# A cross-attention block on one core: another order of the steps that lead into the steady loop

## The chip, the cores and the metric

The kernel runs on one core of a Trainium2 chip. A core has five engines that run side by side, each through its own queue of instructions in order: TensorE (PE, with its weight loads PEld), VectorE (DVE), ScalarE (ACT), GpSimd (POOL) and SyncE (SP), which here only issues DMA transfers. An instruction that has to wait for another engine holds up everything behind it in its own queue. The metric is the device time of the whole kernel in microseconds (us).

## What is computed

Sixteen images x of 1024 rows and 512 features attend to 64 context rows each. All in 32-bit floats:

```python
def _ada_ln(x, c, W_ss, b_ss):
    mu = jnp.mean(x, axis=-1, keepdims=True)
    var = jnp.mean((x - mu) ** 2, axis=-1, keepdims=True)
    h = (x - mu) / jnp.sqrt(var + EPS)
    ss = jax.nn.silu(c) @ W_ss + b_ss
    scale, bias = jnp.split(ss, 2, axis=-1)
    return (1.0 + scale)[:, None, :] * h + bias[:, None, :]
xq = _ada_ln(x_q, t_vec, Wss_q, bss_q)
xkv = _ada_ln(x_kv, t_vec, Wss_kv, bss_kv)
q = (xq @ Wq + bq).reshape(B, Lq, nh, dh)
kv = (xkv @ Wkv + bkv).reshape(B, Lkv, 2, nh, dh)
k, v = kv[:, :, 0], kv[:, :, 1]
scores = jnp.einsum('bqhd,bkhd->bhqk', q, k) / jnp.sqrt(jnp.float32(dh))
attn = jax.nn.softmax(scores, axis=-1)
out = jnp.einsum('bhqk,bkhd->bqhd', attn, v).reshape(B, Lq, H)
return x_q + (out @ Wp + bp)
```

There are 16 heads of 32 features.

## The kernel before

**Blocks.** The rows of x are cut into 32 blocks of 512 rows; a block is four tiles of 128 rows. The context is handled in two groups, "A" and "B", of eight images (512 context rows) each. The three dense layers (query, key and value, output) are computed as products of half-size matrices with seven products in place of eight: `query_product(i, n)`, `context_product(g, "k" or "v", n)` and `product(i, n)` stand for product n of 1 to 7, each four matmul calls (L521, L937). For this the kernel forms sums and differences of weight halves (`column_sums`, `weight_sums`, on POOL) and of feature halves (`feature_sums`, `row_sums`, mostly on POOL). Block 0 is projected without this, by `project_seeded` (L868).

**One block's way.** `load_x` brings the block (SP); `q_stats` (DVE) and `q_scale` (ACT and POOL) make mean and inverse deviation; `hidden` normalises it (ACT); `turn` transposes 32x32 squares (DVE, into the tile `ht`, of which there is one); `move` exchanges the squares between partitions by sixteen transfers from `ht` to `xt` on SP's queue (for block 1, with `two=True`, eight on SP and eight on POOL); `scale_features` applies the conditioning (ACT, four steps). Then the seven query products (PE) and `query_out` (ACT) and `query_added` (DVE) take the query to `qt`, a single buffer. `score_products(i, z)` makes the scores of one half z of the keys into two double banks of PSUM; `maximum` (DVE) and `copied` (ACT) take them out, and only then can the next half go there. `maxima` spreads the row maxima (`mb`), `subtract` (POOL), `weights` (ACT, the exponential), `total` (POOL) and `row_total` (DVE) follow; `inverse_rows` takes the inverse sums through DRAM (`ltd`) back in another order (`vr`) by five small transfers on SP; `spread_rows` and `divided` (DVE) apply them to the result of `mix` (PE), and `product` with `added`, or for block 0 `project_seeded` with `projected`, project it, add it to the residual that `load_residual` brought, and store it. Seeds of the projection's banks are written by ACT (`project_seed`, `biased`).

**The first block and the context** take shorter ways: block 0 and the context rows are transposed on PE (`turned_products`, `turned_features`), and the context is scaled by `modulated` (half on DVE, half on ACT). The conditioning itself comes from `scale_shift_rows`, `scale_shift_taken` and `scale_shift`, with `biases` transposing the bias rows. Values are stored to a stage and brought to their place by `value_move`, eight transfers each.

**The order** is written out by hand, step by step, from L992 on: 410 steps up to L1402, then a loop over the blocks 3 to 29 (L1404), then the last blocks. No scheduler moves anything: a step's instructions go to the end of each engine's queue in the order of the calls. Buffers are shared by tags with few copies: the tag "x" has two for the rows of x, and "r" two for the residuals, which at first hold the value weights and their sums (L159 and L160); a load into a buffer waits for its last reader.

Of the kernel before, what the change touches and what calls it, by code (L numbers as in the profile page):

```python
# [20 lines left out]
def cross_attention_block(  # L21
# [18 lines left out]
    nc = tc.nc  # L40
# [289 lines left out]
    def q_scale(i):  # L330
        apart = i != "A"
        q_rstd[i] = rstd_of(q_mv.pop(i), NT, apart)
# [669 lines left out]
    column_sums("k", w_k_sb, w_k_sums, (2,))  # L1002
    turned_features("A", 0)
    scale_shift_taken("kv", 0)
    hidden("A", (2,))
    column_sums("k", w_k_sb, w_k_sums, (0,))
    turned_features("A", 1)
    turned_features("A", 2)
    scale_shift("kv", 2 * NC, 0)
    column_sums("v", w_v_sb, wv_sums, (2,))  # L1010
    column_sums("v", w_v_sb, wv_sums, (0,))
    turned_features("A", 3)
    modulated("A", 0, 0, nc.scalar)
    load_x("B")
    column_sums("k", w_k_sb, w_k_sums, (1,))
    column_sums("v", w_v_sb, wv_sums, (1,))
    modulated("A", 0, 0, nc.vector)
    scale_shift_rows("kv", 1)
    modulated("A", 0, 1, nc.scalar)
    context_product("A", "k", 1)  # L1020
    column_sums("v", w_v_sb, wv_sums, (3,))
    scale_shift_taken("kv", 1)
    column_sums("k", w_k_sb, w_k_sums, (3,))
    modulated("A", 0, 1, nc.vector)
    scale_shift("kv", 2 * NC, 1)
    modulated("A", 1, 0, nc.vector)
    modulated("A", 1, 0, nc.scalar)
    modulated("A", 1, 1, nc.vector)
    modulated("A", 1, 1, nc.scalar)
    context_out("A", "k", 1)  # L1030
    context_product("A", "v", 1)
    context_product("A", "k", 2)
    context_out("A", "v", 1)
    feature_sums("A", nc.vector, (0,))
    context_out("A", "k", 2)
    feature_sums("A", nc.vector, (1,))
    load_query_weights()
    context_product("A", "v", 2)
    context_out("A", "v", 2)
    feature_sums("A", nc.vector, (2,))  # L1040
    context_product("A", "k", 7)
    feature_sums("A", nc.vector, (3,))
    context_product("A", "v", 7)
    context_out("A", "v", 7)
    context_product("A", "k", 6)
    q_stats(0, (0,))
    context_product("A", "v", 6)
    q_stats(0, (1,))
    context_out("A", "k", 7)
    context_out("A", "k", 6)  # L1050
    q_stats(0, (2,))
    q_stats(0, (3,))
    q_stats("B", (0,))
    q_scale(0)
    scale_shift_rows("q", 0)
    hidden(0, (0,))
    scale_shift_rows("q", 1)
    context_product("A", "k", 5)
    q_stats("B", (1,))
    hidden(0, (1,))  # L1060
    context_out("A", "v", 6)
    context_product("A", "k", 4)
    context_product("A", "v", 5)
    column_sums("q", w_q_sb, w_q_sums, (0,))
    hidden(0, (2,))
    hidden(0, (3,))
    load_x(1)
    q_stats("B", (2,))
    scale_shift_taken("q", 0, 2)
    q_stats("B", (3,))  # L1070
    q_scale("B")
    hidden("B", (1,))
    scale_shift("q", 0, 0, 2)
    context_out("A", "k", 5)
    turned_products()
    turned_scaled(0)
    hidden("B", (0,))
    turned_scaled(3)
    turned_scaled(1)
    turned_scaled(2)  # L1080
    context_product("A", "k", 3)
    context_out("A", "v", 5)
    feature_sums(0, nc.gpsimd, (0,))
    hidden("B", (2,))
    load_projection_bias()
    column_sums("q", w_q_sb, w_q_sums, (2,))
    context_product("A", "v", 4)
    context_out("A", "k", 3)
    hidden("B", (3,))
    turned_features("B", 0)  # L1090
    modulated("B", 0, 0, nc.vector)
    turned_features("B", 1)
    context_product("A", "v", 3)
    turned_features("B", 2)
    modulated("B", 1, 0, nc.scalar)
    feature_sums(0, nc.gpsimd, (1,))
    context_out("A", "k", 4)
    column_sums("q", w_q_sb, w_q_sums, (1,))
    query_product(0, 1)
    modulated("B", 0, 0, nc.scalar)  # L1100
    query_seed(0)
    turned_features("B", 3)
    q_stats(1, (0,))
    q_stats(1, (1,))
    context_out("A", "v", 3)
    feature_sums(0, nc.gpsimd, (2,))
    q_stats(1, (2,))
    load_x(2)
    modulated("B", 0, 1, nc.scalar)
    q_stats(1, (3,))  # L1110
    load_projection()
    query_product(0, 2)
    context_product("B", "k", 1)
    feature_sums(0, nc.gpsimd, (3,))
    column_sums("q", w_q_sb, w_q_sums, (3,))
    query_product(0, 6)
    modulated("B", 1, 1, nc.scalar)
    context_out("A", "v", 4)
    modulated("B", 0, 1, nc.vector)
    modulated("B", 1, 1, nc.vector)  # L1120
    q_scale(1)
    modulated("B", 1, 0, nc.vector)
    query_out(0, 2)
    feature_sums("B", nc.gpsimd, (0,))
    context_out("B", "k", 1)
    hidden(1, (0,))
    feature_sums("B", nc.gpsimd, (1,))
    query_product(0, 7)
    context_product("B", "k", 2)
# [9 lines left out]
    query_out(0, 6)  # L1139
    load_x(3)  # L1140
    context_out("B", "k", 2)
    q_stats(2, (0,))
    query_out(0, 7)
    q_stats(2, (1,))
    move(1, two=True)
    q_stats(2, (2,))
    context_product("B", "k", 6)
    context_out("B", "k", 6)
    query_product(0, 5)
    query_product(0, 4)  # L1150
    value_move("A", 0)
    q_stats(2, (3,))
    query_added(0, 5)
    q_stats(3, (0,))
    q_stats(3, (1,))
    q_scale(2)
    query_product(0, 3)
    value_move("A", 1)
    context_product("B", "k", 7)
    context_product("B", "k", 5)  # L1160
    q_stats(3, (2,))
    query_added(0, 4)
    hidden(2, (0,))
    hidden(2, (1,))
    hidden(2, (2,))
    query_out(0, 3)
    context_out("B", "k", 7)
    q_stats(3, (3,))
    hidden(2, (3,))
    turn(2, (0,))  # L1170
    load_x(4)
    turn(2, (1,))
    turn(2, (2,))
    scale_features(1, (0,))
    nc.gpsimd.tensor_tensor(b_diff, b_second, b_first, ALU.subtract)
    scale_features(1, (3,))
    scale_features(1, (2,))
    scale_features(1, (1,))
    feature_sums(1, nc.gpsimd, (0,))
    feature_sums(1, nc.gpsimd, (1,))  # L1180
    score_products(0, 0)
    context_product("B", "k", 4)
    maximum(0, 0, 0)
    context_out("B", "k", 5)
    query_product(1, 1)
    copied(0, 0, 1)
    maximum(0, 0, 1)
    turn(2, (3,))
    copied(0, 0, 0)
    context_out("B", "k", 4)  # L1190
    query_seed(1)
    q_scale(3)
    score_products(0, 1)
    maximum(0, 1, 1)
    context_product("B", "k", 3)
    maximum(0, 1, 0)
    feature_sums(1, nc.gpsimd, (2,))
    hidden(3, (3,))
    query_product(1, 2)
    context_out("B", "k", 3)  # L1200
    context_product("B", "v", 1)
    query_out(1, 2)
    query_product(1, 6)
    move(2)
    copied(0, 1, 0)
    query_product(1, 7)
    context_out("B", "v", 1)
    maxima(0)
    copied(0, 1, 1)
    feature_sums(1, nc.gpsimd, (3,))  # L1210
    context_product("B", "v", 2)
    query_out(1, 6)
    q_stats(4, (0,))
    query_out(1, 7)
    context_out("B", "v", 2)
    context_product("B", "v", 6)
    context_out("B", "v", 6)
    context_product("B", "v", 7)
    subtract(0, zs=(0,))
    q_stats(4, (1,))  # L1220
    subtract(0, zs=(1,))
    hidden(3, (0,))
    hidden(3, (1,))
    weights(0, 0)
    turn(3, (0,))
    weights(0, 1)
    scale_features(2, (1,))
    total(0)
    hidden(3, (2,))
    q_stats(4, (2,))  # L1230
    query_product(1, 5)
    scale_features(2, (3,))
    query_product(1, 4)
    turn(3, (1,))
    scale_features(2, (2,))
    context_product("B", "v", 5)
    query_added(1, 5)
    context_out("B", "v", 7)
    q_stats(4, (3,))
    query_added(1, 4)  # L1240
    scale_features(2, (0,))
    turn(3, (2,))
    context_out("B", "v", 5)
    query_product(1, 3)
    context_product("B", "v", 4)
    load_x(5)
    turn(3, (3,))
    query_out(1, 3)
    feature_sums(2, nc.gpsimd, (0,))
    row_total(0)  # L1250
    inverse_rows(0)
    move(3)
    score_products(1, 0)
    maximum(1, 0, 0)
    copied(1, 0, 1)
    copied(1, 0, 0)
    context_out("B", "v", 4)
    maximum(1, 0, 1)
    query_product(2, 1)
    score_products(1, 1)  # L1260
    maximum(1, 1, 0)
    maximum(1, 1, 1)
    load_residual(1)
    q_scale(4)
    context_product("B", "v", 3)
    load_residual(0)
    query_seed(2)
    maxima(1)
    feature_sums(2, nc.gpsimd, (1,))
    context_out("B", "v", 3)  # L1270
    feature_sums(2, nc.gpsimd, (2,))
    copied(1, 1, 0)
    copied(1, 1, 1)
    project_seed(0, 1)
    query_product(2, 2)
    query_out(2, 2)
    hidden(4, (0,))
    mix(0)
    subtract(1, zs=(0,))
    spread_rows(0)  # L1280
    query_product(2, 6)
    hidden(4, (2,))
    project_seed(0, 0)
    query_out(2, 6)
    hidden(4, (1,))
    value_move("B", 1)
    divided(0)
    q_stats(5, (0,))
    subtract(1, zs=(1,))
    weights(1, 0)  # L1290
    hidden(4, (3,))
    q_stats(5, (1,))
# [320 lines left out]
```

## Time and profile before

| | |
|---|---|
| median of 3 runs | 1034.3 us (1032.55 to 1035.55) |
| profiled execution, first to last instruction | 1029.1 us |
| busy: PE | 1009.3 us (98%) |
| busy: PEld | 763.4 us (74%) |
| busy: DVE | 860.9 us (84%) |
| busy: POOL | 805.9 us (78%) |
| busy: ACT | 638.6 us (62%) |
| moved by DMA | 149.82 MB, mean 146 GB/s |

The profiler took down one execution: each instruction with its engine, its line in the kernel, its start and its end. The page groups them; other views list one engine's instructions in order of time, the waits with what ended them, the transfers from issue to landing, or the busy time in chosen stretches. Times in the views are microseconds from the first instruction on, unless marked ns. A name such as `pq<-xt,w_q_sb` says what is written and what is read; equal names stand for different blocks, since buffer numbers are left out. The granted clock is the share of full speed that TensorE was given.

### The profile page before, as it was taken

How to read it: one execution, taken by the hardware profiler on the slowest of the kernel's cores; microseconds unless marked ns; L12 is line 12 of the kernel's file. 1: busy time of each engine (PE TensorE's matmuls, PEld its weight loads, DVE VectorE, ACT ScalarE, POOL GpSimd, SP SyncE). 2: the span in 40 equal slices, each digit the busy share in tenths (PEclk: the TensorE clock that was granted, in tenths of full speed). 3: DMA queues.
4: the chain of work that ended last, by engine and by line, in shares of the span. 5: the costliest groups of instructions: out<-in, count | busy, mean ns of one | idle time of the engine just before them, and what ended most of it. 6: DMA issues, size and time to landing. Idle time of an engine off the chain costs nothing.

```text
span 1029.1 us, 21212 instructions
## 1 busy us (share of the span) xinstructions
PE 1009.3 (98%) x8077; PEld 763.4 (74%) x8077; DVE 860.9 (84%) x1174; ACT 638.6 (62%) x1025; POOL 805.9 (78%) x518
## 2 busy tenths in 40 slices
PE   8999899999999999999999999999999999999998
PEld 7877556777777777777777778777777777777746
DVE  6686669889888888889898888898888888876795
ACT  3786565666666666667666666666666676665530
POOL 4566687798888888898888888988888888987861
PEclk9999999999999999999999999999999999999999
DMA  9563544444544444445444444445434444335122
GB/s 318 179 188 119 149 122 136 157 157 156 165 155 121 143 128 154 152 152 166 140 134 146 150 133 153 156 159 165 148 110 151 134 154 154 113 125 166 46 85 85
DMA packets 112197, 149.82 MB, mean 146 GB/s; under 512 B 34104, under 2 KB 45392, under 8 KB 112096
## 3 DMA queue, kind: packets, MB, share of 16 engines
q1 hardware_dynamic: 111712, 147.94, 45.3%
q8 instruction: 64, 1.05, 0.4%
q0 software_dynamic: 384, 0.54, 0.3%
q14 instruction: 37, 0.30, 0.1%
HBM read 79.21 MB, written 34.60 MB: 111 GB/s over the span
## 4 chain that ended last, share of the span: by engine, by line
PE 81%; SPq 6%; DMA 5%; DVE 4%; ACT 1%; issue 1%; POOL 1%; DVEq 0%; ACTq 0%; POOLq 0%
PE pp L955 34%; PE pq L539 33%; PE po L826 6%; PE ps L658 6%; SPq L387 4%; DMA ltd<-lt 1%; SPq L631 1%; PE pk_A L539 1%; PE pv_A L539 1%; DMA xt<-ht 1%; DMA r<-in_x_dram 1%; DVE ht L365 1%; DVE lt L762 1%; DMA wss_kv<-in_L_xcond_Wss_kv_dram 1%; DMA x<-in_x_dram 1%
## 5 line engine op out<-in xcount | busy, mean ns | idle before, releaser
L717 POOL TENSOR_TENSOR s<-s,mb 128x2048 f32<-128x2048 f32 x64 | 290.2, 4558 | 129.3 <-DVE mb L704 127.7
L684 ACT COPY s<-ps 128x1024 f32<-128x1024 f32 x128 | 129.4, 1012 | 108.1 <-DVE m L675 64.8
L675 DVE TRANSPOSE_TENSOR_REDUCE m<-ps 128x32 f32<-128x1024 f32 x128 | 150.7, 1213 | 33.6 <-PE ps L658 33.4
L955 PE MATMUL pp<-w_p_sb,ot 128*128 128x256 f32 x720 | 165.6, 379 | 0.5 <-DVE r L979 0.4
L979 DVE TENSOR_TENSOR r<-pp,r 128x512 f32<-128x512 f32 x203 | 131.8, 670 | 30.9 <-PE pp L955 24.3
L578 ACT ACTIVATE qt<-pq,bias_t 128x256 f32<-128x256 f32 x256 | 105.6, 463 | 77.2 <-PE pq L539 77.0
L955 PEld LDWEIGHTS pp<-w_p_sb,ot 128*128 128x128 f32 x720 | 136.6, 190 | 20.5 <-issue 1.6
L723 ACT ACTIVATE s<-s 128x2048 f32<-128x2048 f32 x64 | 122.3, 1911 | 43.8 <-POOL s L717 43.8
L757 POOL TENSOR_TENSOR sum<-s,s 128x2048 f32<-128x2048 f32 x31 | 140.7, 4540 | 7.0 <-ACT s L723 7.0
L955 PEld LDWEIGHTS pp<-WT,s 128*128 128x128 f32 x480 | 86.5, 189 | 57.0 <-issue 37.7
L539 PE MATMUL pq<-xt_sums,w_q_sums 128*128 128x256 f32 x512 | 123.3, 385 | 0.0
L539 PE MATMUL pq<-xt,w_q_sums 128*128 128x256 f32 x512 | 121.1, 379 | 1.6 <-DVE qt L585 1.6
L539 PE MATMUL pq<-xt,w_q_sb 128*128 128x256 f32 x512 | 121.6, 380 | 0.3 <-ACT pq L551 0.2
L539 PEld LDWEIGHTS pq<-xt_sums,w_q_sums 128*128 128x128 f32 x512 | 94.9, 190 | 36.5 <-issue 24.8
L955 PE MATMUL pp<-WT,s 128*128 128x256 f32 x480 | 119.3, 391 | 0.2 <-POOL s L934 0.2
L955 PE MATMUL pp<-WT,ot 128*128 128x256 f32 x480 | 113.6, 379 | 0.6 <-POOL ot L931 0.6
L539 PEld LDWEIGHTS pq<-xt,w_q_sb 128*128 128x128 f32 x512 | 96.8, 190 | 16.4 <-issue 1.7
L539 PEld LDWEIGHTS pq<-xt,w_q_sums 128*128 128x128 f32 x512 | 97.2, 190 | 15.2 <-DVE qt L585 2.0
L955 PEld LDWEIGHTS pp<-WT,ot 128*128 128x128 f32 x480 | 91.0, 190 | 14.1 <-POOL ot L931 1.0
L335 ACT ACTIVATE x<-x,rstdq 128x512 f32<-128x512 f32 x128 | 97.0, 807 | 4.4 <-POOL rstdq L312 4.4
L447 ACT ACTIVATE xt<-xt,ss_q 128x512 f32<-128x512 f32 x124 | 93.9, 808 | 5.1 <-DMA xt<-ht 4.5
L498 POOL TENSOR_TENSOR xt_sums<-xt 128x512 f32<-128x512 f32 x64 | 81.4, 1272 | 14.2 <-ACT xt L447 7.3
(176 smaller groups left out, 1509.8 us busy)
## 6 DMA issues: line engine op xcount, KB each, us to landing
x<-in_x_dram SPq DMA_DIRECT2D x32, 1024.0 KB, 5.5
r<-in_x_dram SPq DMA_DIRECT2D x32, 1024.0 KB, 5.1
xt<-ht SPq DMA_DIRECT2D x488, 64.0 KB, 2.0
out_dram<-r SPq DMA_DIRECT2D x58, 512.0 KB, 3.7
out_dram<-r SPq DMA_DIRECT2D x11, 256.0 KB, 2.2
wss_kv<-in_L_xcond_Wss_kv_dram SPq DMA_DIRECT2D x4, 512.0 KB, 7.3
wss_q<-in_L_xcond_Wss_q_dram SPq DMA_DIRECT2D x4, 512.0 KB, 11.0
vr<-ltd SPq DMA_DIRECT2D x128, 8.0 KB, 1.6
```

The source lines that it names most:

```text
L335: nc.scalar.activation(dst, src, AF.Identity, bias=rstd[:, 1, j : j + 1], scale=rstd[:, 0, j : j + 1])
L447: nc.scalar.activation(xt[:, :, c, :], xt[:, :, c, :], AF.Identity, scale=ss["q"][:, c, b : b + 1], bias=ss["q"][:, NC + c, b : b + 1],)
L498: eng.tensor_tensor(dst, a, b, ALU.subtract)
L539: nc.tensor.matmul(out_, lhsT=lhsT, rhs=rhs, start=new and m == 0 and c == 0, stop=c == HC - 1, skip_group_check=True,)
L578: nc.scalar.activation(dst, src, AF.Identity, bias=bq_t[:, o : o + 1])
L675: nc.vector.tensor_reduce(m_tiles[i][:, z, 2 * e : 2 * e + 2, :], s_banks[i, z][e].rearrange("p r (j a) -> p r j a", a=32), AX.X, ALU.max, ...
L684: nc.scalar.copy(s_tiles[i, z][:, 2 * e : 2 * e + 2, :], s_banks[i, z][e])
L717: eng.tensor_tensor(s_tiles[i, z], s_tiles[i, z], mb_tiles[i], ALU.subtract)
L723: nc.scalar.activation(p, p, AF.Exp, scale=SCALE)
L757: nc.gpsimd.tensor_tensor(t, s_tiles[i, 0], s_tiles[i, 1], ALU.add)
L955: nc.tensor.matmul(acc[k][:, t * HO : (t + 1) * HO], lhsT=rows[:, c, t * P : (t + 1) * P], rhs=cols[:, c, :], start=n == 2 and t == 0 and ...
L979: nc.vector.tensor_add(r, a, r)
```

## The change

All functions stay as they are, and so do the loads ahead of L992, the loop and the end. The 410 steps from L992 to L1402 are the same calls with the same arguments; about 380 of them stand in another order. So each engine gets the same instructions, in another order in this stretch, and SP's transfers too. The places that the prediction speaks of, cut from a longer diff:

```diff
     q_stats("A", (3,))
+    column_sums("k", w_k_sb, w_k_sums, (0,))
+    biases()
     q_scale("A")
+    hidden("A", (0,))
+    hidden("A", (2,))
+    scale_shift_rows("kv", 0)
+    turned_features("A", 0)
...
-    hidden("A", (1,))
-    scale_shift_rows("kv", 0)
-    biases()
-    hidden("A", (0,))
...
+    context_product("A", "k", 1)
+    scale_shift_rows("kv", 1)
...
+    scale_shift("q", 0, 0, 2)
...
+    context_product("A", "v", 5)
...
+    load_x(1)
+    context_out("A", "v", 5)
+    turned_products()
+    context_product("A", "k", 4)
...
+    context_product("A", "k", 5)
...
     hidden(1, (0,))
+    modulated("B", 1, 0, nc.vector)
+    query_product(0, 6)
+    q_stats(2, (0,))
+    feature_sums("B", nc.gpsimd, (0,))
+    modulated("B", 1, 0, nc.scalar)
...
+    turn(1, (0,))
+    hidden(1, (3,))
+    context_product("B", "k", 2)
+    query_out(0, 7)
+    hidden(1, (1,))
...
+    turn(1, (1,))
...
+    query_out(0, 6)
+    q_stats(2, (2,))
+    hidden(1, (2,))
+    turn(1, (2,))
...
+    turn(1, (3,))
...
+    q_scale(2)
...
+    move(1, two=True)
...
-    hidden(1, (1,))
-    feature_sums("B", nc.gpsimd, (3,))
-    hidden(1, (2,))
-    hidden(1, (3,))
-    turn(1, (0,))
-    turn(1, (1,))
-    turn(1, (2,))
-    turn(1, (3,))
...
-    move(1, two=True)
...
+    score_products(0, 0)
+    scale_features(1, (2,))
+    context_out("B", "k", 5)
+    maximum(0, 0, 0)
+    context_product("B", "k", 4)
+    scale_features(1, (0,))
     turn(2, (1,))
     query_product(1, 1)
     copied(0, 0, 1)
+    scale_features(1, (3,))
+    feature_sums(1, nc.gpsimd, (0,))
+    context_product("B", "k", 3)
...
     score_products(0, 1)
...
+    load_projection()
...
+    score_products(1, 0)
+    query_seed(2)
+    row_total(0)
+    context_product("B", "v", 3)
+    context_product("B", "v", 4)
     scale_features(2, (3,))
+    inverse_rows(0)
+    maximum(1, 0, 1)
+    copied(1, 0, 0)
+    copied(1, 0, 1)
+    load_residual(0)
     scale_features(2, (2,))
+    maximum(1, 0, 0)
+    score_products(1, 1)
...
     move(3)
...
-    score_products(1, 0)
-    maximum(1, 0, 0)
...
-    query_product(2, 1)
-    score_products(1, 1)
...
-    load_residual(1)
...
-    load_residual(0)
...
+    mix(0)
+    load_residual(1)
...
+    score_products(2, 0)
+    q_scale(5)
+    row_total(1)
...
+    query_product(3, 1)
+    copied(2, 0, 1)
+    project_seeded(0, 2)
...
+    inverse_rows(1)
...
+    load_x(6)
+    score_products(2, 1)
     projected(0, 1)
...
+    move(4)
...
-    projected(0, 1)
...
-    load_x(6)
...
-    inverse_rows(1)
-    score_products(2, 0)
...
-    move(4)
...
+    added(1, 2)
+    biased(1, 3)
     turn(5, (0,))
+    query_added(3, 4)
+    turn(5, (1,))
...
+    load_x(7)
+    move(5)
     product(1, 7)
```

More of the change, by code (lines that the diff above doesn't have):

```diff
@@ L1028, in cross_attention_block @@
[L1028 to L1042, printed above, removed]
@@ L1078, in cross_attention_block @@
     turned_scaled(3)
[L1079 to L1088, printed above, removed]
+    column_sums("q", w_q_sb, w_q_sums, (3,))
+    load_x(2)
     hidden("B", (3,))
@@ L1091, in cross_attention_block @@
     modulated("B", 0, 0, nc.vector)
+    turned_features("B", 2)
+    q_stats(1, (3,))
+    hidden("B", (1,))
     turned_features("B", 1)
[L1093 to L1098, printed above, removed]
-    query_product(0, 1)
[L1100 to L1104, printed above, removed]
@@ L1105, in cross_attention_block @@
-    context_out("A", "v", 3)
-    feature_sums(0, nc.gpsimd, (2,))
-    q_stats(1, (2,))
[L1108 to L1118, printed above, removed]
+    context_out("A", "k", 3)
+    turned_features("B", 3)
+    context_out("A", "v", 4)
@@ L1226, in cross_attention_block @@
-    weights(0, 1)
+    context_product("B", "v", 7)
+    subtract(0, zs=(1,))
+    load_x(5)
+    weights(0, 1)
+    query_added(1, 5)
+    q_stats(4, (3,))
+    total(0)
+    context_out("B", "v", 7)
+    hidden(3, (3,))
+    turn(3, (0,))
+    context_out("B", "v", 6)
+    turn(3, (1,))
+    query_product(1, 3)
+    query_product(1, 4)
+    turn(3, (2,))
+    scale_features(2, (0,))
+    query_out(1, 3)
     scale_features(2, (1,))
-    total(0)
-    hidden(3, (2,))
     q_stats(4, (2,))
-    query_product(1, 5)
@@ new lines, in cross_attention_block @@
+    query_out(3, 2)
+    projected(0, 3)
+    weight_sums()
+    q_stats(6, (0,))
+    query_out(3, 6)
+    query_product(3, 7)
+    q_stats(6, (1,))
+    subtract(2, zs=(0,))
+    query_product(3, 5)
+    q_stats(6, (2,))
+    query_out(3, 7)
+    biased(1, 2)
+    product(1, 1)
+    weights(2, 0)
+    subtract(2, zs=(1,))
+    row_sums(1, 0)
+    weights(2, 1)
+    query_product(3, 4)
+    hidden(5, (3,))
+    product(1, 2)
+    query_added(3, 5)
+    q_stats(6, (3,))
+    hidden(5, (0,))
+    total(2)
```

457 lines of the change are left out of this document (208 added, 249 removed).

## The prediction

> **What bounds the kernel now.** I read the stretches first: the way in (0 to 162.6, where the steady loop's first score product starts), the loop's first pass, and the loop behind it. The columns after the length are busy us (instructions) of PE, PEld, DVE, ACT and POOL, the granted clock, the DMA share and GB/s.
>
> ```profile
> span 1029.1 us, 21212 instructions
> ...
> 0.00:162.60 162.60, 150.11 (x1045) 113.78 (x1045) 116.37 (x218) 103.48 (x204) 105.93 (x97) 0.99 0.58 177
> 162.60:200.00 37.40, 36.05 (x322) 26.22 (x323) 31.58 (x41) 22.10 (x34) 29.04 (x20) 1.00 0.48 158
> 200.00:960.00 760.00, 760.00 (x6247) 580.97 (x6246) 665.15 (x866) 493.85 (x767) 634.21 (x388) 1.00 0.45 144
> ```
>
> From 200 to 960 PE is busy for all 760 us, at full clock. The change leaves the loop and PE's amount of work as they are, so the end moves by as much as PE's idle and slowed time before 200 moves: 12.5 us before 162.6, 1.4 behind it. The timeline of PE shows where it lies; the bracket is the idle time before a row and what ended it.
>
> ```profile
> 12.11 1.53 PE L400 MATMUL pxk_A<-ident,x_A 128*128 128x128 f32 x12 [0.93 <-DVE x_A L344]
> ...
> 37.85 1.72 PE L430 MATMUL pxt<-ident,x 128*128 128x128 f32 x14 [0.45 <-DVE ss_q L284]
> ...
> 73.06 1.47 PE L658 MATMUL ps<-qt,K_A 32*32 32x512 f32 x32 [0.24 <-ACT s L684]
> ...
> 101.63 1.77 PE L658 MATMUL ps<-qt,K_A 32*32 32x512 f32 x32 [1.46 <-ACT s L684]
> ...
> 128.08 5.40 PE L871 MATMUL pp<-w_p_sb,ot 128*128 128x512 f32 x8 [2.92 <-ACT pp L866]
> ...
> 137.11 1.18 PE L658 MATMUL ps<-qt,K_A 32*32 32x512 f32 x32 [0.64 <-ACT s L684]
> ...
> 140.05 3.60 PE L871 MATMUL pp<-w_p_sb,ot 128*128 128x512 f32 x8
> ...
> 158.28 1.99 PE L539 MATMUL pq<-xt,w_q_sums 128*128 128x256 f32 x8 [1.64 <-DVE qt L585]
> ...
> 162.62 1.51 PE L658 MATMUL ps<-qt,K_A 32*32 32x512 f32 x32 [0.62 <-ACT qt L578]
> ...
> 188.40 1.97 PE L539 MATMUL pq<-xt_sums,w_q_sb 128*128 128x256 f32 x8 [1.33 <-ACT qt L578]
> ```
>
> The largest is at 128.08: PE idles 2.92 us, and the same eight matmuls that take 3.60 at 140.05 then take 5.40. Together 4.7 us.
>
> **The change, part by part.** I lay each engine's new queue end to end with the durations above and below. A product (eight records) has a slot of 1.74 us in the chain of waits. Negative is a gain.
>
> ```profile
> 46.06 1.74 PE pq L539 x8
> ```
>
> *A, the start.* Biases now stand ahead of the first scale-shift rows and of the statistics' scale.
>
> ```profile
> 10.94 0.24 PE L234 MATMUL pb<-ident,early 24*128 24x24 f32 x1
> ```
>
> ```profile
> 11.22 0.18 DVE L235 COPY bias_t<-pb 128x24 f32<-128x24 f32 x1 [1.69 <-PE pb L234]
> ...
> 11.51 0.54 DVE L344 TENSOR_SCALAR x_A<-x_A,rstdq 128x512 f32<-128x512 f32 x1
> ```
>
> DVE sat 1.69 us for `pb`, and so normalised the first context rows late, for which PE waited 0.93. Moved ahead, `pb` falls where PE waits for weights anyway: −0.9. Given back: product 1 of the keys now stands ahead of the second scale-shift rows, reaches its modulated features about 0.5 too early, and those rows with their DVE copy lie open for some 0.35. Net −0.1, between −0.9 and +0.9.
>
> *B, products of context group A in another order.* Value product 5 now lies between the transposed scales and `pxt`, and hides DVE's addition: of 0.45 I keep 0.15 for the last row of x, normalised just then. Net −0.3, between −0.45 and +1. The column sums on POOL are the same six, in another order ahead of the products that use them; were one late, it would cost its own length at most.
>
> *C, x_1's way to its features.* Here the new order loses.
>
> ```profile
> 53.80 2.83 DVE L365 STREAM_TRANSPOSE ht<-x 128x512 f32<-128x512 f32 x4 [0.67 <-ACT x L335]
> ```
>
> ```profile
> 57.07 5.61 SPq L387 DMA_DIRECT2D xt<-ht  x8
> ```
>
> ```profile
> DMA to landing us min/median/max: 5.3/5.6/6.1
> ```
>
> ```profile
> 58.19 4.03 POOL L387 DMA_DIRECT2D xt<-ht  x8
> ```
>
> ```profile
> 52.96 2.93 ACT L335 ACTIVATE x<-x,rstdq 128x512 f32<-128x512 f32 x4
> ...
> 55.78 0.82 ACT L578 ACTIVATE qt<-pq,bias_t 128x256 f32<-128x256 f32 x2
> ...
> 68.27 2.93 ACT L447 ACTIVATE xt<-xt,ss_q 128x512 f32<-128x512 f32 x4 [0.59 <-DMA V_A<-stage_A]
> ```
>
> ```profile
> L421 ACT ACTIVATE xk_B<-pxk_B,ss_kv 128x64 f32<-128x64 f32 x16 | 5.0, 433 | 0.0
> ```
>
> Before, ACT normalises the four rows of x_1 in one go. Now one modulation of four instructions (a quarter of 5.0) and two query outputs (0.82 each) stand between them: 2.9 us later for the last transpose on DVE, at about 59.5 instead of 56.6. Behind it queue x_3's load and `move(1)` on SP; POOL's half has the next rows' scale ahead too. The last of SP's eight issues starts near 62.1 and lands within 6.1, at 68.2, just when ACT's scaling begins (68.27). Shifted by 2.9 that is 71.2. Three scalings at 0.73 come before x_1's first product can run (the order is now 1, 2, 0): 73.4. PE gets there, behind the first score half and one key product, at about 70. A wait of 3.3, between 0 (lands by 67.8) and 4.5. And a slowed clock, as at 128.08:
>
> ```profile
> 128.00:130.00 2.00, 1.92 (x4) 0.98 (x5) 2.00 (x2) 1.96 (x5) 0.00 (x0) 0.87 0.65 204
> 130.00:132.00 2.00, 2.00 (x4) 0.68 (x3) 1.89 (x4) 1.21 (x5) 1.26 (x5) 0.50 0.44 106
> ```
>
> The 2.92 us of idling there were followed by a granted clock of 0.50, at a price of 5.40 − 3.60 = 1.8; the 1.46 at 101.63 by none. I take the drop: +3.3 + 1.8 = +5.1.
> The Trainium skill ("TensorE: Matmul & The Clock Gate", section "What's actually happening") has the clock halve after an idle window of about 3.4 us that runs free of the kernel, so that a gap just below it may pass unpunished. This trace halved after 2.92 us; by the rule's lenient end the 1.8 would not fall due, a rival below.
>
> *D, the pairs of score halves.* The second half needs the first one's banks, read by two maxima on DVE and two copies on ACT.
>
> ```profile
> L675 DVE TRANSPOSE_TENSOR_REDUCE m<-ps 128x32 f32<-128x1024 f32 x12 | 14.4, 1224 | 4.2 <-PE ps L658 4.0
> ...
> L762 DVE TRANSPOSE_TENSOR_REDUCE lt<-sum 128x64 f32<-128x2048 f32 x3 | 6.9, 2291 | 0.0
> ```
>
> Between the halves now stand two products (blocks 0 and 1; before two and one) and a product with a projection (block 2; before one product). That ends waits of 0.24 and 1.46 (block 2's under F). Given back: block 1's maxima queue behind a row total of 2.29 that C has delayed, 0.5 left; and `mix(0)` comes two products after the second half instead of three, while DVE still has two maxima of 1.22 and one statistic: 0.7. Net −0.5, between −1.7 and +2.
>
> *E, residual loads.*
>
> ```profile
> 104.97 10.65 SPq L387 DMA_DIRECT2D xt<-ht  x16
> 115.73 1.10 SPq L126 DMA_DIRECT2D r<-in_x_dram  x2
> ```
>
> ```profile
> 116.36 10.26 DMA r<-in_x_dram
> 126.71 0.69 DVE r L882
> ```
>
> The residual of block 0 was issued behind the sixteen moves of `move(3)` and behind block 1's, landed at 126.6, and held the projection's addition on DVE, the seed on ACT and PE. Now it goes ahead of `move(3)`, alone: some 11 us earlier. Even at 10.26 us it lands near 118; the first projection ends only near 120. −2.92 − 1.80 = −4.7. The load waits for the buffer of the value sums, free after value product 3, which stands earlier on PE than the inverse sums' landing. The bias, weight and x loads also moved lie under SP's other waits; the projection's weights, the latest, now go near 90 and are used near 117:
>
> ```profile
> w_p_sb<-in_L_xcond_Wp_dram SPq DMA_DIRECT2D x1, 1024.0 KB, 7.6
> ```
>
>
> *F, the loop's entry.*
>
> ```profile
> 99.45 3.37 DMA ltd<-lt
> ...
> 135.41 5.16 DMA ltd<-lt
> ```
>
> ```profile
> 142.43 10.91 SPq L387 DMA_DIRECT2D xt<-ht  x16
> ```
>
> ```profile
> 155.09 1.31 DVE L365 STREAM_TRANSPOSE ht<-x 128x512 f32<-128x512 f32 x2 [4.61 <-DMA xt<-ht]
> ```
>
> Block 1's inverse sums took 5.16 us to DRAM right behind x_6's megabyte, against 3.37 at 99.45, and came late because their row total queued behind the projection of E. `move(4)` came after, and DVE's next transposes waited for it until 155.09; the query's additions behind them gave PE's 1.64 and 0.62. Now x_6 follows the inverse sums, and one addition precedes the transposes. By the queues `move(4)` starts near 139 (before 142.4), against an entry 3 to 4 earlier. −0.64 − 1.64 − 0.62 = −2.9; between −2.9 and +0.8 (all of it back, with the slip of the list that follows).
>
> *G, the first pass.* `move(5)` comes some 5 to 6 earlier, PE 3.6: of 1.33 I take −0.8, between −1.3 and +1.
>
> Sum: −0.1 − 0.3 + 5.1 − 0.5 − 4.7 − 2.9 − 0.8 = −4.2. The profiled span of 1029.1 becomes 1024.9. The median of the runs, 1034.3, lies 5.2 above that span; I take the same distance: 1030.1.
>
> **The rivals.**
>
> 1. *C's wait comes without the slow clock*: 1.8 less, −6.0, 1028.3. For it: one gap, one drop is all the trace shows; against it, that gap was shorter.
> 2. *C's wait does not come*, because the moves land before PE arrives, as they would where x_3's megabyte and the values' transfers didn't share the engines with them: −4.2 − 5.1 = −9.3, 1025.0.
> 3. *The reorder does less than it says*: swaps between engines change no queue, and F and G stay. Block 1's residual now stands directly ahead of the values' sixteen transfers, which before waited for residuals to land; the inverse sums of block 1 still queue behind them. Without F and G: −4.2 + 3.7 = −0.5, 1033.8.
>
> ```profile
> SPq L631 <- DMA r<-in_x_dram: 5.0, 2, 4.4
> ```
>
> 4. *Slower: C's delay runs down SP's queue.* x_3, `move(1)`, the values' transfers, x_4 and `move(2)` are one queue; the first maxima, the subtraction on POOL, the total and the inverse sums hang on the second score half. If no slack takes it up, `move(4)` starts 2.9 later than before, and the moves, not PE, set the entry at 165.5: +2.9, 1037.2. It decides if `move(4)`'s first issue falls after 142.4. Against it: the inverse sums of block 1 lose two delays of their own (F), E's projection and x_6.
>
> **How the numbers follow.** Chances: forecast 0.35 (own range 1028.5 to 1031.2), rival 1 0.15, rival 2 0.12, rival 3 0.20, rival 4 0.18. Three thousandths are 3.1 us, about what can be told from no change; the forecast and rivals 1 and 2 lie beyond it on the fast side: 0.62; rival 3 within: 0.20; rival 4 0.18. The range of 8 in 10 leaves out the far half of rival 2 and the tail of rival 4: 1025 to 1037.5.
>
> **What would show it.** PE's timeline: no wait at L400 for `x_A` and none at L871 for the seed (A, E); a wait of about 3 us at x_1's first product, released by ACT's scaling, with a granted clock of 0.5 behind it (C); the second score halves of blocks 1 and 2 waiting under 0.6 (D); block 0's residual issued ahead of sixteen moves near 107 (E); `move(4)` near 139 and the first loop score near 158 (F). Wrong it is if PE idles over 1 us at a place not named here between 20 and 160, or if that first loop score comes at 162 or later.

## The result, and the profile after

| | before | changed |
|---|---|---|
| median of 20 runs each, side by side | 1032.7 us (1030.2 to 1035.6) | 1029.3 us (1028.1 to 1031.8) |
| ratio, 95% interval | | 0.9968 (0.9961 to 0.9976) |
| profiled execution, span | 1029.1 us | 1027.3 us |
| first score product of the steady loop starts at | 162.62 us | 160.10 us |

The change makes the kernel 3.4 us faster (0.0032 × 1032.7 = 3.3 by the ratio). The two profiled executions differ by 1.8 only; where the other 1.6 are comes out below.

The stretches of the changed kernel, with the columns as before (length; busy us of PE, PEld, DVE, ACT, POOL; granted clock, DMA share, GB/s):

```profile
span 1027.3 us, 21213 instructions
...
0.00:160.10 160.10, 148.60 (x1045) 113.57 (x1046) 114.79 (x217) 102.91 (x199) 102.70 (x95) 0.99 0.62 181
160.10:200.00 39.90, 38.26 (x334) 28.25 (x334) 35.08 (x44) 24.06 (x41) 32.52 (x25) 1.00 0.49 147
200.00:960.00 760.00, 759.87 (x6244) 580.63 (x6243) 665.02 (x866) 495.26 (x767) 635.73 (x385) 1.00 0.47 144
```

PE stays the bound behind 200. Ahead of the loop its idle time fell only from 12.5 to 11.5 us (160.10 − 148.60), and its busy time from 150.1 to 148.6. The timeline of PE in the changed kernel shows that the waits are other ones than before:

```profile
10.30 1.07 PE L256 MATMUL ps_kv<-wss_kv,early 128*32 128x128 f32 x28 [1.00 <-DMA wss_kv<-in_L_xcond_Wss_kv_dram]
...
13.61 1.09 PE L400 MATMUL pxk_A<-ident,x_A 128*128 128x128 f32 x8 [1.08 <-DVE xk_A L419]
...
17.85 0.33 PE L278 MATMUL ps_kv<-ident,early 128*128 128x128 f32 x1 [0.41 <-DVE early L269]
...
47.08 1.53 PE L400 MATMUL pxk_B<-ident,x_B 128*128 128x128 f32 x12 [1.34 <-DVE xk_B L419]
...
76.79 3.03 PE L539 MATMUL pq<-xt,w_q_sb 128*128 128x256 f32 x8 [4.45 <-ACT xt L447]
79.62 2.58 PE L539 MATMUL pk_B<-xk_B,w_k_sums 128*128 128x256 f32 x8
...
112.80 2.37 PE L826 MATMUL po<-s,V_A 32*32 32x512 f32 x64 [0.45 <-ACT s L684]
...
122.12 3.60 PE L871 MATMUL pp<-w_p_sb,ot 128*128 128x512 f32 x8
...
160.10 1.33 PE L658 MATMUL ps<-qt,K_A 32*32 32x512 f32 x32
...
186.11 1.97 PE L539 MATMUL pq<-xt_sums,w_q_sb 128*128 128x256 f32 x8 [1.39 <-ACT qt L578]
```

Gone are 0.93 for `x_A`, 0.45 for the transposed scales, the 2.92 at the projection with its slowed clock, all three waits of second score halves (0.24, 1.46, 0.64), and 1.64 and 0.62 at the loop's entry. New are 1.08 and 0.41 in group A, 1.34 in group B, 4.45 at x_1's first product with a slowed clock behind it (3.03 and 2.58 for two products that take 1.89 to 1.99 elsewhere), and 0.45 at `mix(0)`. At 186 the 1.33 of before is still there, as 1.39.

The busy time fell too. Products that follow a wait can take longer themselves: two of the three second score halves that waited before took 1.47 and 1.77 us, the third 1.18; without a wait a score half ahead of the loop takes 1.14 to 1.22. The group of all score products went from 7.8 us in the kernel before, first row, to 7.0 in the changed one, second row (us in total, mean ns of one, and the idle time ahead of them). The mean of a single one is the same, so they overlapped less, which is about half of the 1.5 us:

```profile
L658 PE MATMUL ps<-qt,K_A 32*32 32x512 f32 x192 | 7.8, 600 | 2.3 <-ACT s L684 2.3
```

```profile
L658 PE MATMUL ps<-qt,K_A 32*32 32x512 f32 x192 | 7.0, 599 | 0.0
```

SP's queue in the changed kernel (start, length from first to last issue) bears on the steps C, E, F and G:

```profile
48.69 13.73 SPq L119 DMA_DIRECT2D x<-in_x_dram  x2
62.47 6.50 SPq L387 DMA_DIRECT2D xt<-ht  x8
69.02 11.45 SPq L631 DMA_DIRECT2D V_A<-stage_A  x16
...
110.43 0.39 SPq L126 DMA_DIRECT2D r<-in_x_dram  x1
111.17 10.93 SPq L387 DMA_DIRECT2D xt<-ht  x16
122.20 0.52 SPq L126 DMA_DIRECT2D r<-in_x_dram  x1
...
140.86 12.43 SPq L387 DMA_DIRECT2D xt<-ht  x16
...
166.71 0.43 SPq L119 DMA_DIRECT2D x<-in_x_dram  x1
167.24 12.97 SPq L387 DMA_DIRECT2D xt<-ht  x16
```

Block 0's residual goes ahead of `move(3)`, as the diff says (before: 115.73, behind it). `move(1)` starts at 62.47 in place of 57.07, right behind x_3's megabyte; `move(4)` at 140.86 in place of 142.43; `move(5)` at 167.24 in place of 171.59, but takes 12.97 us in place of 10.93.

### The profile page after: what moved, and what is told of

It is laid out like the page before. It is cut to its first block, busy times and chain, and to the rows that moved or that the text cites. A ratio compares the mean times of both kernels' runs of the same rounds, so it can differ in the third digit from the quotient of the medians.

```text
span 1027.3 us, 21213 instructions
## 1 busy us (share of the span) xinstructions
PE 1008.1 (98%) x8077; PEld 763.3 (74%) x8077; DVE 860.8 (84%) x1174; ACT 639.7 (62%) x1025; POOL 805.9 (78%) x518
## 4 chain that ended last, share of the span: by engine, by line
PE 88%; DMA 3%; DVE 3%; ACT 2%; SPq 1%; issue 1%; POOL 1%; DVEq 0%; ACTq 0%; POOLq 0%
PE pq L539 36%; PE pp L955 34%; PE ps L658 6%; PE po L826 6%; PE pp L871 1%; PE pv_B L539 1%; DMA x<-in_x_dram 1%; PE pv_A L539 1%; DMA xt<-ht 1%; PE pk_A L539 1%; DMA wss_kv<-in_L_xcond_Wss_kv_dram 1%; SPq L387 1%; DVE m L675 1%; ACT s L723 1%; ACT xk_B L421 0%
```

## The experiments

Each kernel was timed beside the kernel before on the same chip. The ratio to before follows its time, with the 95% interval; differences in us are worked out from the ratios with 1032.7. The kernel of experiment 6 is called kernel 6, and so on.

**1. E alone on the kernel before.**

```diff
     inverse_rows(0)
+    load_residual(0)
     move(3)
...
-    load_residual(1)
...
-    load_residual(0)
...
     mix(0)
+    load_residual(1)
```

> The kernel before, with step E alone: block 0's residual is loaded ahead of move(3), block 1's behind mix(0). Theory 1 (PE's idle and slowed time simply adds up): the 2.92 us wait at the first projection and the 1.80 us of the slowed clock behind it go, and the time falls by 4 to 4.7 us, to about 1028.3. Theory 2 (block 3's and 4's moves set the loop's entry): the same 4.7 us go at the projection, but move(4) still starts within 1.5 us of 142.4, the waits at the loop's entry (1.64 + 0.62 us before) grow by 2 to 4 us, and the whole falls by 0 to 2 us. What tells them apart is the start of the first loop score product: 158 by theory 1, 161 or later by theory 2.

1028.1 us, 0.9967 (0.9955 to 0.998): −3.4 us, a little under the 4 to 4.7 expected. In the profile none of block 0's projections waits any more, and the loop's first score product starts at 158.06, 4.6 us earlier: theory 1. (That execution was the shortest of the ten, and other waits moved in it too: 0.48 in place of 1.46 at block 1's second score half, and a new 0.54 at 144.86.) The waits at the entry stay, and the one behind it is longer, 1.93 in place of 1.33 (PE's timeline of this kernel):

```profile
153.72 1.99 PE L539 MATMUL pq<-xt,w_q_sums 128*128 128x256 f32 x8 [1.72 <-DVE qt L585]
158.06 1.51 PE L658 MATMUL ps<-qt,K_A 32*32 32x512 f32 x32 [0.62 <-ACT qt L578]
184.44 1.97 PE L539 MATMUL pq<-xt_sums,w_q_sb 128*128 128x256 f32 x8 [1.93 <-ACT qt L578]
```

So two moved loads, out of 380 moved steps, give as much as the whole change.

**2. C undone on the changed kernel.**

```diff
-    hidden(1, (0,))
...
     modulated("B", 1, 0, nc.scalar)
+    hidden(1, (0,))
+    hidden(1, (3,))
+    hidden(1, (1,))
+    hidden(1, (2,))
...
     context_product("B", "k", 6)
+    move(1, two=True)
     q_scale(2)
```

> The changed kernel with step C undone: the four rows of x_1 are normalised in a row again, behind one modulation, and move(1) stands ahead of the next rows' scale. Theory 1 (C's price is PE's 4.45 us of waiting and some 1.7 of slowed clock, and all of it reaches the end): the wait at x_1's first query product falls below 1.5 us, no granted clock of 0.5 follows, and the time falls by 4 to 6 us against the changed kernel. Theory 2 (move(4) and move(5) set the end): the wait goes, but at most 2 us reach the end, the rest comes back as waits between 150 and 190. Theory 3 (the landing of the moves, not their issue, is late, because x_3's megabyte and the values' transfers share the engines): the wait stays above 2.5 us.

1026.4 us, 0.9943 (0.993 to 0.9956): some 2.6 us faster than the changed kernel. But the edit didn't undo all of C: DVE still had the next rows' statistics between the four transposes. ACT had normalised the last row at 59.32 (changed kernel: 60.64), but DVE ended its last transpose at 62.13 (61.98), so `move(1)` started at 62.62 (62.47) and ACT's scaling at 74.30, as late as in the changed kernel (74.52). What changed is where PE waited (its timeline):

```profile
60.20 1.97 PE L539 MATMUL pq<-xt_sums,w_q_sb 128*128 128x256 f32 x8 [1.08 <-ACT qt L578]
...
72.34 1.51 PE L658 MATMUL ps<-qt,K_A 32*32 32x512 f32 x32 [1.20 <-ACT qt L578]
...
76.58 1.99 PE L539 MATMUL pq<-xt,w_q_sb 128*128 128x256 f32 x8 [0.80 <-ACT xt L447]
```

One wait of 4.45 became three that add up to 3.08, and no slowed clock follows. The transfers were late as before; PE just didn't stand still long enough in one piece.

**3. x_3's load behind `move(1)`** (`load_x(3)` moved from behind `query_product(0, 2)` to behind `move(1, two=True)`).

> The changed kernel with the load of x_3 issued behind move(1) in place of ahead of it. If x_3's megabyte, issued just ahead, is what stretches SP's half of move(1) from 5.61 to 6.50 us and its landing, ACT's scaling of x_1 begins 1 to 3 us earlier than 74.5 and the wait of 4.45 us shrinks by as much, and the time by 1 to 3 us. If not, the wait stays within 0.5 us of 4.45, and block 3's statistics come later than before, with no gain at the end (0 to +1 us).

1031.5 us, 0.999 (0.9981 to 1.0): 2.3 us slower than the changed kernel. The first half of the expectation held: SP's half of `move(1)` took 5.04 us in place of 6.50, its transfers landed 3.0 us after their issue in place of 6.7 (medians), ACT's scaling of x_1 began at 70.74 in place of 74.52, and x_1's product waited 0.46. But x_3 came so late that DVE stood 11.35 us for its statistics, and the addition to the keys queued behind them. DVE's row first, then PE's:

```profile
75.45 0.69 DVE L294 BATCH_NORM_STATS2 bs<-x 128x6 f32<-128x512 f32 x1 [11.35 <-DMA x<-in_x_dram]
```

```profile
79.87 3.78 PE L539 MATMUL pk_B<-xk_B,w_k_sums 128*128 128x256 f32 x8 [4.86 <-DVE K_B L605]
```

**4. x_7's load behind `move(5)`** (the two steps exchanged).

> The changed kernel with the load of x_7 issued behind move(5) in place of ahead of it. If that megabyte, directly ahead, is why move(5)'s sixteen issues took 12.97 us in place of 10.93 and why G was not gained, move(5) takes about 11 us, ACT's scaling of block 5 begins near 180 in place of 181.9, the wait of 1.39 us at 186 goes, and the time falls by 1.0 to 1.4 us. If the sixteen issues take their time from something else, the wait stays at 1.0 to 1.4 us and the time is the same within 0.5 us.

1033.7 us, 1.0014 (1.0004 to 1.0024): 4.8 us slower than the changed kernel. `move(5)` took 10.01 us, the shortest of all kernels here; but x_7, issued 11 us later (178.06 against 166.71), made DVE stand 5.35 us for its rows, with the query's additions behind them, and PE waited 3.19 us at 190.81, with a slowed clock. With x_7 ahead, `move(5)` took anything from 10.67 to 12.97 us in the other kernels with this loop entry, so whether and how much the load stretches the move stays open.

**5. DVE's first modulations behind the transposes again.**

```diff
-    modulated("A", 0, 0, nc.vector)
     turned_features("A", 2)
     turned_features("A", 3)
+    modulated("A", 0, 0, nc.vector)
...
-    modulated("B", 0, 0, nc.vector)
     turned_features("B", 2)
...
     turned_features("B", 3)
+    modulated("B", 0, 0, nc.vector)
```

> The changed kernel with DVE's first modulation of each context group behind the transposes of tiles 2 and 3 again, in place of ahead of tile 2's. Theory 1: the waits of 1.08 and 1.34 us before tile 2's transposes come from there alone (the two tiles share a bank, and PE may not write while DVE's modulation has not read), so both go, and since ACT's half of the context and x_1 behind it come earlier, the 4.45 us at x_1's first product shrink too: 2 to 4 us faster than the changed kernel. Theory 2: the waits move on to the first products, which need the same features: 1.08 and 1.34 come back as waits at those products, and the time is the same within 0.7 us.

1027.4 us, 0.995 (0.9937 to 0.9963): 1.9 us faster than the changed kernel, just under theory 1's range. In group B the 1.34 is gone; in group A the 1.08 came back as 0.95, now for ACT's modulation of tile 1 ahead of tile 3:

```profile
13.98 0.66 PE L400 MATMUL pxk_A<-ident,x_A 128*128 128x128 f32 x4 [0.95 <-ACT xk_A L421]
...
75.30 3.65 PE L539 MATMUL pq<-xt,w_q_sb 128*128 128x256 f32 x8 [4.78 <-DMA V_A<-stage_A]
```

The wait at x_1's product didn't shrink, though theory 1 had it so: ACT, the moves and PE all came some 1.5 us earlier.

**6. The first 200 steps as before, the rest as changed** (A, B, C and block 0's score pair undone; the other 207 steps in the changed order; the first steps that differ from before stand behind step 204).

> The first 200 steps in the order of before (so A, B, C and block 0's score pairs undone), the other 207 in the changed order (block 1's and 2's score pairs, E, F, G). If PE's idle and slowed times add: E's 4.0 us as measured alone, and 2 to 3.5 us of F and G, so 6 to 7.5 us faster than before, with the first loop score product at about 155. If the moves set the entry as soon as E is there (theory 2): less than 1 us beyond E, with waits of more than 2 us between 145 and 190.

1023.0 us, 0.991 (0.9896 to 0.9924): −9.3 us, more than the 6 to 7.5 expected; the waits add up, as in the first theory. The loop's first score product starts at 153.95, and behind 80 us PE has only these waits of over 0.2 us left:

```profile
106.64 2.38 PE L826 MATMUL po<-s,V_A 32*32 32x512 f32 x64 [0.48 <-ACT s L684]
...
159.19 1.17 PE L658 MATMUL ps<-qt,K_A 32*32 32x512 f32 x32 [0.25 <-ACT s L684]
...
179.38 1.97 PE L539 MATMUL pq<-xt_sums,w_q_sb 128*128 128x256 f32 x8 [0.81 <-ACT qt L578]
```

The changed order behind step 200 is worth nearly three times the whole change.

**7. The first 126 steps as before, the rest as changed** (A and B undone, C in).

> The first 126 steps (start and group A and B, so A and B undone) in the order of before, the rest in the changed order, C among it. If C alone makes the loss, the wait at x_1's first product and the slowed clock are there as in the changed kernel (4 to 6 us together), and the time is 4 to 6 us above that of the kernel that keeps 200 steps of before, about 1029 to 1031. If a part of C's 4.45 us came from the start (ACT's half of group B held up by tile 2's transposes), the wait is nearer the 3.3 us that were forecast, or below, and the time lies 2 to 4 us above it.

1028.0 us, 0.9956 (0.9944 to 0.9969): −4.5 us, so C, with block 0's score pair, costs 9.3 − 4.5 = 4.8. The wait is 3.75, between the 3.3 forecast and the 4.45 of the changed kernel; and the clock halves in the midst of it. PE's timeline, and below it the granted clock in the last column but two:

```profile
75.00 3.78 PE L539 MATMUL pq<-xt,w_q_sb 128*128 128x256 f32 x8 [3.75 <-ACT xt L447]
78.57 2.74 PE L539 MATMUL pk_B<-xk_B,w_k_sums 128*128 128x256 f32 x8
```

```profile
74.00:76.00 2.00, 1.00 (x2) 0.84 (x3) 2.00 (x4) 2.00 (x4) 0.00 (x0) 0.50 0.29 70
76.00:78.00 2.00, 2.00 (x6) 1.63 (x5) 1.97 (x4) 1.95 (x4) 1.27 (x1) 0.50 0.42 103
78.00:80.00 2.00, 2.00 (x6) 1.55 (x6) 1.61 (x3) 1.06 (x4) 1.12 (x5) 0.50 0.38 92
80.00:82.00 2.00, 2.00 (x38) 1.08 (x36) 0.00 (x0) 0.00 (x0) 1.92 (x2) 0.93 0.46 71
```

**8. E with F and G alone**: the kernel of experiment 1 up to step 314, the changed order behind it.

> Before with E, and behind step 314 the changed order (F and G alone, with block 2's score pair). If F is worth what was forecast (-2.9) and G half of its wait (-0.8), the three waits at the entry (0.64, 1.72, 0.62 us with E alone) go, and it is 2.5 to 3.7 us faster than with E alone. If the chain of move(4) and move(5) takes over, the waits turn up again at 150 to 190 and the gain over E alone is 0 to 1 us.

1028.5 us (1025.25 to 1029.99), 0.9953 (0.9934 to 0.9971): the times lie too far apart to tell a gain over E alone. The trace tells more: from 135 to 200 PE has only one wait of over 0.2 us, 0.25, so F's waits and G's are gone, while two that experiment 1 doesn't have stand at block 2's first score half and in the product behind it (0.56 and 0.67). And in this execution block 1's second score half, whose steps are those of experiment 1, waited 1.95 us (there 0.48) and met a halved clock, which takes back what F gives:

```profile
103.44 2.64 PE L658 MATMUL ps<-qt,K_A 32*32 32x512 f32 x32 [1.95 <-ACT s L684]
106.02 3.78 PE L539 MATMUL pv_B<-wv_sums,xk_B 128*128 128x256 f32 x8
...
130.40 1.51 PE L658 MATMUL ps<-qt,K_A 32*32 32x512 f32 x32 [0.56 <-ACT qt L578]
...
133.21 1.56 PE L539 MATMUL pq<-xt,w_q_sb 128*128 128x256 f32 x6 [0.67 <-ACT xt L447]
```

The mean granted clock of each execution points the same way. The two of the six at 1.000 took 1025.3 and 1025.9 us; of E alone, eight of ten were at 1.000, with a median of 1027.7. So where no slowed clock falls in, F and G look worth some 2 us, from two executions only.

**9 and 10. The two parts of C, one at a time, on kernel 6.** First ACT's: the modulation and two query outputs between x_1's rows.

```diff
     hidden(1, (0,))
+    modulated("B", 1, 0, nc.scalar)
...
     hidden(1, (1,))
+    query_out(0, 7)
...
     hidden(1, (2,))
+    query_out(0, 6)
     hidden(1, (3,))
```

> The kernel with the first 200 steps of before, and ACT's part of C alone on it: one modulation of group B and two query outputs stand between the four normalisations of x_1 again, all else in place. Theory 1 (ACT's delay is C, as forecast): the last transpose of x_1 comes 2.5 to 3 us later, move(1) too, the wait at x_1's first product (0.73 us) grows to about 3, a granted clock of 0.5 follows, and the time rises by 3 to 5 us against the kernel with 200 steps of before, to 1026 to 1028. Theory 2 (it is POOL's half): the wait stays under 1.5 us and the time within 1 us.

1026.5 us (1024.56 to 1029.15), 0.9945 (0.9927 to 0.9963): 3.6 us slower than kernel 6. The profiled execution, the fastest of the six, shows `move(1)` at 60.00 (kernel 6: 57.76), the scaling at 71.67 (69.54), PE waits of 0.71 and 1.42 and no slowed clock. Theory 1 in its direction, though the wait is half of the 3 us expected. The slower five had mean granted clocks of 0.997 to 0.999, the profiled one 1.000, so a slowed stretch in those is likely; where it lies, no profile shows.

Then POOL's: `move(1)` behind the next rows' scale.

```diff
-    move(1, two=True)
     q_stats(2, (2,))
+    q_stats(2, (3,))
+    q_scale(2)
+    move(1, two=True)
```

> The kernel with the first 200 steps of before, with move(1) behind the scale of the next rows (q_scale(2)), so that POOL's eight transfers follow those four small operations and the statistics they need, SP's eight too; ACT's order of x_1's rows as before. Theory 1 (ACT's delay is C): SP's half and POOL's start at most 2 to 3 us later in POOL, the wait at x_1's first product grows by less than 1.5 us and the time by 0 to 1.5 us. Theory 2 (POOL's half, queued behind the scale, is C): POOL's half starts near 62.5 in place of 58.9, the wait grows to about 3 to 4 us, and the time by 3 to 5 us.

1022.6 us, 0.9904 (0.9888 to 0.992): as kernel 6. POOL's half started 4.9 us later (63.81 against 58.88), but its transfers landed 2.5 us after their issue in place of 6.2 (medians), and x_1's product waited 0.27 (0.73). So POOL's half is not what C costs. ACT's order alone costs 3.6 of the 4.8, known to about 2.4. The third thing that C moves, DVE's statistics between the transposes (experiment 2), was not tried alone.

**11. The good half of A on kernel 6**: `biases()` ahead of `q_scale("A")`, nothing else.

> The kernel with the first 200 steps of before, with the biases alone moved ahead of the first scale-shift rows and of the statistics' scale, the good half of A. If the forecast of A's first half holds, DVE no longer sits behind the biases, the wait of 0.93 us at the first context transposes goes, and it is 0.5 to 0.9 us faster, about 1022.3. If DVE's next reader waits for the same weights anyway, the 0.93 comes back as another wait before 20 us and the time is the same within 0.4 us.

1022.4 us, 0.99 (0.9883 to 0.9917): not told apart from kernel 6 by its time. The 0.93 is gone, with 0.17, 0.32 (normalised rows) and 0.33 (weights from DRAM) in its place. A wait of 1.19 at 24.22 for the keys' addition is there too, but one of 1.00 stands at the same place in kernel 10, whose start is kernel 6's, so it belongs to the execution and not to the edit. Kernels 6, 10 and 11 are the fastest seen, some 6 to 7 us ahead of the changed kernel.

**12. The kernel before, profiled a second time.**

> The kernel before, profiled a second time, because its runs spread over 1030.2 to 1036.3 us while its first profile, 1029.1 us long, belongs to the fast end. Theory 1 (the clock): where this execution takes over 1032 us, it shows one more stretch of 3.4 or 6.8 us at a granted clock of 0.5 than the first one, most likely behind the second score half of block 1 near 101, whose wait (1.46 us then) is the longest one without a drop; where it takes under 1031.5 us it shows only the stretch near 130. Theory 2 (elsewhere): the longer time lies in the loop or its end, with the same PE waits and the same clock before 200.

This execution took 1035.4 us, with a span of 1033.6, 4.5 above the first. Of these, 3.2 are there at the loop's first score product (165.84 against 162.62). PE's timeline:

```profile
103.81 1.97 PE L658 MATMUL ps<-qt,K_A 32*32 32x512 f32 x32 [2.07 <-ACT s L684]
105.70 3.44 PE L539 MATMUL pv_B<-wv_sums,xk_B 128*128 128x256 f32 x8
...
130.82 3.70 PE L871 MATMUL pp<-w_p_sb,ot 128*128 128x512 f32 x8 [1.84 <-ACT pp L866]
...
152.76 3.48 PE L955 MATMUL pp<-w_p_sb,ot 128*128 128x256 f32 x8 [2.14 <-DVE ot L806]
```

The same program has other waits in another execution: 2.07 us in place of 1.46 at block 1's second score half, now with a halved clock behind it (3.44 for a product that took 1.99 before), 1.84 in place of 2.92 at the projection, without one, and a new 2.14 at 152.76, with one (3.48; 1.97 in experiment 1). That is one more slow stretch than in the first profile, and at the place named: theory 1. Not foreseen was that the one near 130 would be missing and one would come at 153. And the clock is at most half of the 4.5 us: PE was busy 2.3 us longer (1011.6 against 1009.3), which holds the slower products, and idle 2.1 us longer.

## Why the prediction was right, and where it was not

The forecast of 1030.1, 4.2 below the 1034.3 given, is met within 0.8 by the time (1029.3) and by the difference (−3.4). The terms, by the kernels that separate them:

| terms | forecast | measured | from |
|---|---|---|---|
| E | −4.7 | −3.4 (−4.6 to −2.1) | 1 |
| D for blocks 1 and 2, F, G | −4.0 | −5.9 | 6 less 1 |
| C, and D for block 0 | +4.9 | +4.8 | 7 less 6 |
| A, B | −0.4 | +1.2 | changed less 7 |
| sum | −4.2 | −3.3 | |

An interval of ±0.8 (the changed kernel) to ±1.5 (kernel 6) lies on each of these ratios, so a difference of two is known to between 1.5 and 1.9. The row of A and B can't be told from zero by its times alone; the traces bear it out: PE got to x_1's first product at 72.34 in the changed kernel and at 71.25 in kernel 7 (start of the product less its wait).

That the sum came within 0.9 is in part luck: E gave 1.3 less than forecast and A and B came out 1.6 worse, while D, F and G gave 1.9 more.

*E* went as written: no wait at L871, four projections at 3.60 to 3.70, and the entry 4.6 earlier in experiment 1's profile; by the times it is somewhat less.

*C* is right in size, and in its mechanism as far as it goes. The landing was expected at 71.2 with a wait of 3.3 and a slowed clock at 1.8. With the start as before, ACT's scaling began at 72.72 and PE waited 3.75, with some 2.6 for the clock (half of the 5.2 us from 75.0 on that were slow); in the changed kernel 4.45 and 1.7. ACT's order, the stated cause, delays the move on its own (experiment 9); the POOL half, named beside it, does not (experiment 10). What the prediction left out is DVE: the next rows' statistics now stand between the transposes, and with ACT's rows together again they kept `move(1)` just as late (experiment 2). And the delay would not tell without x_3's megabyte, which stands directly ahead of the move in both orders: with it behind, the moves land in time, as rival 2 had it (experiment 3), though the price then falls due at x_3.

*A and B* are the step that failed: the sum saw only what the new order hides. "`pb` falls where PE waits for weights anyway" was right, the 0.93 went, and the 0.35 given back for the second scale-shift rows came as 0.41. What it missed is that DVE's first modulation now stands ahead of the transposes of tile 2. The code gives tiles 0 and 2 the two halves of one PSUM tile (`spares[i, t % 2]`, a double bank), and in the trace PE's write into the second half waits until DVE has read the first: 1.08 in group A. In group B DVE's modulation itself came late, behind statistics that waited for x_1's landing, and PE waited 1.34, from 45.74 to 47.08. DVE's timeline in the changed kernel:

```profile
43.94 0.69 DVE L294 BATCH_NORM_STATS2 bs<-x 128x6 f32<-128x512 f32 x1 [1.28 <-DMA x<-in_x_dram]
...
45.94 1.09 DVE L419 TENSOR_SCALAR xk_B<-pxk_B,ss_kv 128x64 f32<-128x64 f32 x4
```

Experiment 5 takes the order back and 1.9 us with it, known to about 1.5. By the prediction's own test, PE idle for over 1 us between 20 and 160 at a place not named, group B's 1.34 made this part wrong.

*D, F and G* together gave more than forecast. D ended all waits of second halves; its 0.7 at `mix(0)` came as 0.45, its 0.5 for block 1 didn't come. What the sum lacked is that a wait can cost more than its bracket: the product behind it may be longer (1.47 and 1.77 against 1.18), and in some executions the clock halves, as in experiments 8 and 12. F held: the three waits are gone wherever the changed order stands behind step 314, and `move(4)` and the entry came at 140.9 and 160.1, near the 139 and 158 forecast. G, taken at −0.8, gave nothing in the changed kernel (1.39), 0.5 in kernel 6 (0.81) and all of it in experiment 8. Why it differs stays open: the last issue of `move(5)` came 18.4 us after the loop's first score product in kernel 6 and 18.7 in experiment 8, where nothing waited. D, F and G were not measured one by one.

*The base* was misread, with little harm. The 5.2 us between the first profile's span and the median were taken as a fixed distance. In the experiments an execution takes 1.7 to 1.9 us more than its span (experiment 12: 1035.4 against 1033.6). So the first profile was of one of the shorter executions, at about 1030.9, and the rest of the 5.2 is the spread of the runs. Against that profile the change gains 1.8, against the median 3.4; the latter includes waits that the first profile didn't show at their usual length.

*The rivals.* Rival 1 (no slow clock) fell: it is there in the changed kernel and in experiment 7. Rival 2 (no wait) fell. Rival 3 (F and G stay) fell for F and held for G. Rival 4 (`move(4)` after 142.4) fell at 140.86, with 1.5 us to spare.

## What to carry to other kernels

Split a large reorder at points where both orders have issued nearly the same steps, and measure first half and second half apart: here the second half was worth −9.3 us and the first gave 6 back. Before moving a reader or a load, look at what shares its buffer and at what stands behind it in its queue, since both x loads put later freed a move and then held up DVE for 5 and 11 us. Do the sum against more than one profiled execution when the runs spread by more than the gain in question.

## What the hardware showed that was not expected

**The clock halves after shorter waits than 2.92 us too, and for a fixed length of time or twice that.** Read in steps of 0.4 us, the slow stretches were 3.4 us long (the changed kernel, from 77.6 to 81.0; experiment 4, from 191.6 to 195.0) or twice that (experiment 7, from 73.4 to 80.2; experiment 8, from 103.5 to 110.3). They came after waits of 1.95 and 2.07 us as well as 4.45; waits of 1.93 (experiment 1, at 184) and 1.84 (experiment 12, at 130) passed without. Here is the one of experiment 12, where the clock falls some 1.4 us after PE is back at work (the last column but two):

```profile
102.00:104.00 2.00, 0.19 (x8) 0.18 (x16) 2.00 (x3) 1.34 (x4) 0.00 (x0) 1.00 1.02 395
104.00:106.00 2.00, 2.00 (x33) 0.48 (x18) 1.43 (x2) 1.25 (x5) 0.97 (x5) 0.81 0.10 29
106.00:108.00 2.00, 2.00 (x6) 1.55 (x5) 1.93 (x4) 1.59 (x2) 1.92 (x2) 0.50 0.17 16
108.00:110.00 2.00, 2.00 (x9) 1.75 (x8) 2.00 (x2) 0.92 (x2) 0.39 (x1) 0.83 0.29 70
```

The Trainium skill ("TensorE: Matmul & The Clock Gate", section "What's actually happening") has a window of about 3.4 us that runs free of the kernel, and a halved clock after at least one idle window. The length agrees with every stretch read here, once or twice over, and so does a fall that doesn't coincide with the wait. That a whole window must be idle does not: 1.95 us were enough. Which waits are hit changes from one execution to the next, as the two profiles of the kernel before show, and this kernel with several waits of about 2 us spreads more: by 3.6 to 6.7 us each time it was measured here with ten runs or more. Kernel 6, whose longest wait is 0.93 once its first load has landed, spread by 2.2 in five runs. The clock is not all of it: of 78 executions of the kernel before with a known mean granted clock, the 42 at 0.998 lie between 1030.1 and 1034.5 us, and the four at 1.000 between 1030.7 and 1032.7.
